# The start of a two-layer network: bias rows straight from the input, their loads on SyncE, flips first, values behind scores

## The chip, the cores and the metric

The kernel runs on one core of a Trainium2 chip. The metric is device time in microseconds (us); lower is better. In the engine names of the profile PE is TensorE, DVE is VectorE, ACT is ScalarE, POOL is GpSimd and SP is SyncE, which computes nothing and issues most of the DMAs.

## The reference

The input is an image batch `x` of shape (2, 128, 64, 64): two images, 128 channels, 64 x 64 pixels, float32. It goes through two layers.

```python
# layer 0: group norm, then a block with 7x7 neighbourhood attention
x = x + _L0_conv_ref(_gn(x), ...)
# layer 1: full attention over the 4096 tokens, then spectral convolutions
t = _to_tokens(x)
t = t + _L1_attn_ref(_ln_t(t))
t = t + _L1_ffn_ref(_ln_t(t), ...)
x = _from_tokens(t, x)
```

The change concerns the start of layer 0. Inside it:

```python
y = _ln(x, g1, be1)
qkv = (y @ qkv_w.T + qkv_b)...          # 4 heads of 32
attn = einsum('bnhwd,bnhwijd->bnhwij', q, Kw)   # 49 neighbours of each pixel
attn = attn + rpb[:, bih, biw]          # learned bias by relative position, one table a head
attn = softmax(attn)
out = einsum('bnhwij,bnhwijd->bnhwd', attn, Vw) @ proj_w.T + proj_b
y = _ln(out, g2, be2) @ w1.T + bl1;  x = y + r
y = relu(_ln(x, g3, be3) @ w2.T + bl2);  y = _ln(y, g4, be4) @ w3.T + bl3;  x = y + r
```

`rpb` is a table of 13 x 13 biases for each of the four heads; a pixel at the border has its neighbourhood shifted inside the image, so that the same table is read at other offsets there.

## The kernel before

**Bands.** Layer 0 works on 16 bands, eight per image; a band is 8 rows of 64 pixels, that is 512 tokens. In a band the 64 pixels of an 8 x 8 tile attend to a window of 14 x 14 pixels (196 keys) around it, with a mask for the pairs that are no neighbours. Two tiles make a unit, and a band has four units u0 to u3.

**Pieces.** The work of a band is cut into named pieces. The preparation pieces begin with `p.`: `xg` applies the group norm (L453), `tok` transposes to tokens on PE (L344), `bn`, `pw`, `nb`, `zd`, `za` make the layer norm, `tr` (L202) and `zT` (L445) turn the normed tokens back, `q` and `k` are linears on PE (L349) with their copies `qT` (ACT, L468) and `kT` (DVE, L477), and `v` (PE, L483) with its copy `vc` (ACT, L491) makes the values. A unit's pieces are `S`, the scores on PE (L523); `t0` to `t3`, per head the addition of the bias table together with a minimum on DVE (L536); `e0` to `e3`, the exponentials on ACT (L546); `T` and `c`, transposes of the probabilities (PE L559) and their copies (L566); and `V`, the product with the windows of the values (PE L581).

**Values through DRAM.** A window of 14 x 14 pixels reaches into neighbouring bands, so the values go through a DRAM buffer `vd`. The piece `vc` writes the band's eight tiles there (L493, eight DMAs of 32 KB), and `windows` reads, for every unit, four pieces of 98 pixels into a tile `vw` (L510, 49 KB each, six tiles in rotation). The windows of a band can be completed only when the next band's values are stored. All of these DMAs are issued by SP.

**Order.** The pieces have due times: a dictionary `PLAN` gives one to each piece name, and band k adds k * `PERIOD` (2300). The pieces are emitted in the order of due time. For the start there is a list `FIRST`: what stands in it gets its position minus 1000 as due time, so all of it comes ahead of u0.S of the first band (due at 0). Everything that PE, DVE, ACT and POOL do is then executed in the written order, each engine for itself; SP's DMAs are ordered by a scheduler, by when they can go. A ring of five PSUM banks serves linears, flips, values, scores and transposes in written order.

**The bias table.** The table comes in padded, as `rpb_pad`, with 22 rows of 70 numbers for each head. The kernel copies it to a DRAM scratch `rpb` that has six more rows ahead (two DMAs on ACT's queue, L306 and L307). It then loads, for each head, 64 partitions that start at consecutive offsets, 1350 numbers each, 337.5 KB in all (L310, `rev[h]`; four DMAs on ACT's queue; heads 0 and 3 lie in the space named `tt`, heads 1 and 2 in `cm`). `flipped(h)`, listed as f0 to f3, multiplies with a reversed identity to turn the order of partitions (PE L269, two products of 400 columns) and copies the result to `base` (ACT L273). `table` subtracts it from the mask: 196 keys per row, for six cases of border by four heads. The first case is done on DVE (tab0 to tab3, L278), the others on POOL (`tab`).

**The first loads.** SP loads image 0 in four parts (`xa`, L136), the weights (L284 to L286) and the mask (L301, 588 KB).

Layer 1 follows: attention from about 340 us to 1000 us, the convolutions from there to the end.

Of the kernel before, what the change touches and what calls it, by code (L numbers as in the profile page):

```python
# [8 lines left out]
F32 = mybir.dt.float32  # L9
AF = mybir.ActivationFunctionType  # L10
ALU = mybir.AluOpType
# [9 lines left out]
HEADS, DH, KW = 4, 32, 7  # L21
# [5 lines left out]
DIAG = -1.0e6  # L27
# [8 lines left out]
RPW = 70  # L36


QT, WN, NTAB = 8, 14, 20
# [5 lines left out]
RPR = NTAB + 2  # L45
RLEN = (NTAB - 1) * RPW + NTAB
# [25 lines left out]
PERIOD = 2300  # L72


FIRST = (
    "gn p.xg0 p.xg1 p.tok0 p.tok1 w f0 f1 p.bn0 p.bn1 p.pw0 p.pw1 x1 p.zd0 p.nb0 p.za0 p.tr0 p.zd1 p.nb1 p.za1 wd p.xg2"
    " p.zT0 f2 p.tr1 f3 tab p.zT1 p.v0 p.q0 p.k0 p.vc0 p.qT0 tab0 tab1 tab2 p.kT0 tab3 p.v1 p.k1 p.q1 p.vc1 p.kT1 p.qT1"
).split()
PHW = P + TH


# [21 lines left out]
def kernel(  # L103
# [16 lines left out]
    nc = tc.nc  # L120
# [4 lines left out]
    first_ = ExitStack()  # L125
# [9 lines left out]
    for c in range(4):  # L135
# [10 lines left out]
    space = tok[0].rearrange("p n c -> p (n c)")  # L146
# [3 lines left out]
    rev = [place[:, 0 : NTAB * RPW], *(cm[0][0 : QT * QT, h * RLEN : h * RLEN + NTAB * RPW] for h in range(2))]  # L150
    rev.append(place[:, NTAB * RPW : 2 * NTAB * RPW])

    ident = const.tile([P, P], F32, name="ident")
    make_identity(nc, ident)

# [3 lines left out]
        out=flip, in_=flip, compare_op=ALU.not_equal, fill=1.0, base=1 - QT * QT, pattern=[[0, 2], [1, QT * QT]],  # L159
        channel_multiplier=1,  # L160
    )
    ndiag = const.tile([P, P], F32, name="ndiag")
    nc.vector.tensor_scalar(ndiag, ident, DIAG, None, ALU.mult)
    ones = const.tile([1, P], F32, name="ones")
    nc.vector.memset(ones, 1.0)
    mhalf = const.tile([P, KF], F32, name="mhalf")
# [73 lines left out]
    with l0a:  # L240
# [10 lines left out]
        vdram = l0a.enter_context(tc.tile_pool(name="l0_dram", bufs=1, space=bass.MemoryType.DRAM))  # L251
# [3 lines left out]
        w_sb = wp.tile([P, 896], F32, name="w_sb")  # L255
        v_sb = wp.tile([P, 11], F32, name="v_sb")
        r_sb = wp.tile([1, 4, P], F32, name="r_sb")
# [4 lines left out]
        tab = big.tile([P, 6, HEADS, KEYS], F32, name="tab")  # L262
# [12 lines left out]
        def table(ci, h, eng):  # L275
# [5 lines left out]
                    base[hp, h, n0 : n0 + WN, m0 : m0 + WN], ALU.subtract,  # L281
                )

        nc.sync.dma_start(out=w_sb, in_=wT)  # L284
        nc.sync.dma_start(out=v_sb, in_=vecs)
        nc.sync.dma_start(out=r_sb, in_=rows.unsqueeze(0))  # L286


        gavg = wp.tile([P, 32, 4], F32, name="gavg")
        nc.gpsimd.memset(gavg, 0.25)  # L290
        nc.gpsimd.affine_select(
            out=gavg, in_=gavg, compare_op=ALU.is_ge, fill=0.0, base=0,
# [3 lines left out]
            out=gavg, in_=gavg, compare_op=ALU.is_ge, fill=0.0, base=3,  # L296
            pattern=[[4, 32], [0, 4]], channel_multiplier=-1,
        )
        gavg = gavg.rearrange("p g r -> p (g r)")

        nc.sync.dma_start(out=mask, in_=nc.inline_tensor(_window_masks(), "window_masks").ap())  # L301


        rpb = vdram.tile([(6 + HEADS * RPR) * RPW], F32, name="rpb")
        flat = rpb_pad.rearrange("h r w -> (h r w)")
        nc.scalar.dma_start(out=rpb[0 : 6 * RPW], in_=flat[0 : 6 * RPW])  # L306
        nc.scalar.dma_start(out=rpb[6 * RPW :], in_=flat)  # L307
        for h in range(HEADS):
            src = bass.AP(rpb.tensor, rpb.offset + h * RPR * RPW + 50, [[RPW, QT], [1, QT], [1, RLEN]])
            nc.scalar.dma_start(out=rev[h][:, 0:RLEN], in_=src)  # L310
        wg = w_sb
        cb = wp.tile([P, 5], F32, name="cb")
        C_Q, C_K, C_V, C_1, C_3 = range(5)
# [478 lines left out]
        for k, (b, g) in enumerate(order):  # L792
            t = {}
            for name, at in PLAN.items():
                if name[0] == "k" and b == 0:
                    continue

                at = FIRST.index(f"{name}{k}") - 1000 if f"{name}{k}" in FIRST else at + k * PERIOD
                events.append((at, k, name, lambda f=pieces[name], t=t, b=b, g=g: f(t, b, g)))
        def second():  # L800
            for c in range(4):
# [75 lines left out]
    with ap_:  # L877
# [6 lines left out]
        def bank():  # L884
# [6 lines left out]
            out=tr.rearrange("p h e c -> p (h e) c"),  # L891
            in_=nc.inline_tensor(t_in, "t_in").ap().rearrange("(h p) c -> p h c", p=P),
# [565 lines left out]
        for hh in range(SG // 2):  # L1458
            for e in range(2):
                at = 1 + (2 * hh + e) * 2 * LG * KF  # L1460
                pns[hh, e] = zc[0][:, 0, at : at + 2 * LG * KF].rearrange("p (k l f) -> p k l f", k=KF, l=2)
                nc.sync.dma_start(
                    out=pns[hh, e].rearrange("p k l f -> p (k l) f"),
                    in_=bass.AP(
                        phi_pad.tensor, P - FB + (2 * P * hh + e) * FB, [[2 * FB, P], [PHW, 2 * KF], [1, LG]]
                    ),
# [338 lines left out]
def _window_masks():  # L1805

    import numpy as np

    def seen(offset):

        q, k = np.arange(QT)[:, None], np.arange(WN)[None, :]
        lo = np.clip(offset + q - 3, 0, WN - KW)
        return (k >= lo) & (k < lo + KW)

    m = np.zeros((2, QT, QT, 6, WN, WN), np.float32)
    for ci in range(6):
        rows_ = seen((0, 6, 3)[ci // 2])
        for ab in range(2):
            cols = seen(((0, 6), (3, 3))[ci % 2][ab])
            m[ab, :, :, ci] = np.where(rows_[:, None, :, None] & cols[None, :, None, :], 0.0, -MASKED)  # L1820
    return m.reshape(P, 6, KEYS)
# [76 lines left out]
```

## Time and profile before

| what | value |
|---|---|
| median of the three runs shown | 1955.65 us (1949.8, 1955.65, 1957.53) |
| the profiled execution: its own time | 1954.66 us |
| the profiled execution: span | 1952.8 us |
| PE busy | 1891.0 us |
| layer 0, 0 to 340 us | PE busy 15.93 of the first 31 us, 146.91 of the 156 to 187, 147.11 of the 153 to 340 |
| attention, 340 to 1000 us | PE busy 651.86 of 660 us |
| convolutions, 1000 to 1952 us | PE busy 929.21 of 952 us |

The span is the time from the first to the last instruction that the profiler saw; the run's own time holds 1.9 us around it. A row of a timeline has the start in us, the duration, the engine, the line of the kernel, the operation, output<-input, sizes, and how many instructions were put together (x8); square brackets give the idle time just before and what ended it. "SPq" and "ACTq" are the issuing of DMAs by SP and ACT; a row there lasts as long as the issuing does, not as long as the transfer. "PEld" is the loading of weights into PE.

### The profile page before, as it was taken

The page shows a single profiled execution, that of the slowest core. Times are in us where ns is not written, and L with a number is a line of the kernel's source. Part 1 is how long each engine was busy: PE and PEld are TensorE (multiplying, and loading weights), DVE is VectorE, ACT ScalarE, POOL GpSimd, SP SyncE. Part 2 cuts the span into 40 slices and gives each one's busy share as a digit, 9 for nine tenths or more (in the row PEclk, how much of TensorE's full clock was granted, in tenths as well). Part 3 has the DMA queues.
Part 4 walks back from the last instruction along what each step waited for, and adds up shares of the span by engine and source line. Part 5 has one row for each costly group of instructions (what it writes and reads, how often), then busy time and mean ns, then how long its engine had stood idle before and what let it go on. Part 6 is the DMA issues. An engine that isn't in the chain of part 4 may idle for free.

```text
span 1952.8 us, 50772 instructions
## 1 busy us (share of the span) xinstructions
PE 1891.0 (97%) x20440; PEld 1347.5 (69%) x20440; DVE 956.0 (49%) x3026; ACT 731.3 (37%) x1718; POOL 737.7 (38%) x1209
## 2 busy tenths in 40 slices
PE   6899998999999999999999998999999999999997
PEld 3677776444444444444444456999999999999996
DVE  5799997454554534353454373333333333333332
ACT  2789887322233333232333222222222222222221
POOL 4366886424643335532425431122221121222211
PEclk9999999999999999999999999999999999999999
DMA  5222221667776544988867413222222223222211
GB/s 155 63 61 59 62 62 39 153 184 211 228 203 188 156 123 125 261 206 228 247 196 197 127 53 83 67 65 69 66 67 54 59 72 90 66 68 67 67 40 44
DMA packets 249769, 226.14 MB, mean 116 GB/s; under 512 B 126815, under 2 KB 204655, under 8 KB 242112
## 3 DMA queue, kind: packets, MB, share of 16 engines
q1 hardware_dynamic: 222786, 129.15, 27.5%
q10 hardware_dynamic: 8126, 58.04, 7.6%
q0 software_dynamic: 18624, 35.72, 6.3%
q8 instruction: 162, 2.65, 0.6%
q14 instruction: 71, 0.58, 0.1%
HBM read 131.40 MB, written 91.25 MB: 114 GB/s over the span
## 4 chain that ended last, share of the span: by engine, by line
PE 84%; DVE 5%; POOL 4%; DMA 2%; issue 1%; ACT 1%; SPq 0%; ACTq 0%; DVEq 0%; POOLq 0%
PE acc L1620 29%; PE own L984 12%; PE other L1057 9%; PE bank L926 9%; PE pc L1601 7%; PE bank L349 2%; PE bank L935 2%; PE bank L559 2%; PE bank L202 2%; PE bank L1177 1%; PE bank L1221 1%; PE bank L523 1%; ACT p L546 1%; PE po L581 1%; PE pc L1658 1%
## 5 line engine op out<-in xcount | busy, mean ns | idle before, releaser
L1606 DVE COPY y<-pc 128x512 f32<-128x512 f32 x320 | 206.2, 686 | 348.6 <-PE pc L1601 348.3
L1606 ACT COPY y<-pc 128x512 f32<-128x512 f32 x320 | 171.8, 589 | 402.5 <-PE pc L1601 396.9
L1620 PE MATMUL acc<-y,mpl 32*128 32x256 f32 x5120 | 321.6, 379 | 0.8 <-DVE af L1630 0.8
L1620 PE MATMUL acc<-y,mmi 32*128 32x256 f32 x5120 | 313.1, 375 | 0.0
L1620 PEld LDWEIGHTS acc<-y,mpl 32*128 32x128 f32 x5120 | 289.4, 186 | 7.3 <-DVE af L1630 1.7
L1620 PEld LDWEIGHTS acc<-y,mmi 32*128 32x128 f32 x5120 | 290.4, 185 | 2.6
L1631 POOL TENSOR_TENSOR af<-af 128x512 f32<-128x512 f32 x39 | 49.7, 1274 | 573.3 <-DVE af L1630 535.9
L1057 PE MATMUL other<-e,tok 128*128 128x512 f32 x448 | 227.5, 594 | 0.2
L931 ACT ACTIVATE e<-bank 128x512 f32<-128x512 f32 x216 | 129.1, 598 | 252.5 <-PE bank L926 241.8
L926 PE MATMUL bank<-cm 128*128 128x512 f32 x432 | 222.5, 601 | 0.0
L984 PE MATMUL own<-et,tok 128*128 128x512 f32 x448 | 212.1, 598 | 3.3 <-DVE et L974 3.2
L1601 PE MATMUL pc<-ct,ut 32*128 32x256 f32 x2560 | 208.3, 376 | 2.0 <-DVE y L1606 2.0
L1162 POOL TENSOR_TENSOR ub<-uo 128x256 f32<-128x256 f32 (+1 forms) x176 | 111.0, 666 | 176.4 <-ACT uo L1158 148.2
L1601 PEld LDWEIGHTS pc<-ct,ut 32*128 32x128 f32 x2560 | 170.1, 185 | 7.6 <-DVE y L1606 4.1
L974 DVE STREAM_TRANSPOSE et<-et 128x512 f32<-128x512 f32 x216 | 134.2, 678 | 70.9 <-DMA et<-eb 70.8
L984 PEld LDWEIGHTS own<-et,tok 128*128 128x128 f32 x448 | 85.7, 192 | 111.2 <-issue 96.1
L1057 PEld LDWEIGHTS other<-e,tok 128*128 128x128 f32 x448 | 81.5, 191 | 89.6 <-issue 82.1
L926 PEld LDWEIGHTS bank<-cm 128*128 128x128 f32 x432 | 76.3, 191 | 73.9 <-issue 67.7
L546 ACT ACTIVATE p<-p,mn 128x196 f32<-128x196 f32 x256 | 114.3, 449 | 14.4 <-DVE mn L536 13.9
L1093 POOL DMA_DIRECT2D us<-ub x158 | 108.0, 725 | 12.5 <-DMA us<-ub 10.1
L1158 ACT COPY uo<-bank 128x512 f32<-128x512 f32 (+1 forms) x96 | 45.4, 517 | 96.9 <-PE bank L1177 55.2
L1630 DVE COPY af<-acc 128x256 f32<-128x256 f32 x80 | 30.3, 420 | 104.6 <-PE acc L1620 104.6
(269 smaller groups left out, 2625.3 us busy)
## 6 DMA issues: line engine op xcount, KB each, us to landing
eb<-e ACTq DMA_DIRECT2D x54, 1024.0 KB
et<-eb SPq DMA_DIRECT2D x216, 256.0 KB
ut<-us SPq DMA_DIRECT2D x156, 128.0 KB
us<-ub POOLq DMA_DIRECT2D x54, 256.0 KB, 5.2
vw<-vd SPq DMA_DIRECT2D x256, 49.0 KB
ct<-gs SPq DMA_DIRECT2D x312, 40.0 KB
ct<-gs SPq DMA_DIRECT2D x312, 32.0 KB
vd<-v SPq DMA_DIRECT2D x128, 32.0 KB
```

The source lines that it names most:

```text
L546: nc.scalar.activation(p, p, AF.Exp, bias=t[name + "mn"][:, h : h + 1], scale=-1.0, accum_out=t["den"][:, u, h : h + 1],)
L926: nc.tensor.matmul(ps.rearrange("p (q t j) -> p q t j", q=4, t=4), lhsT=cm[b][:, n * P : (n + 1) * P], rhs=keys.rearrange("p (t q j) -> p ...
L931: nc.scalar.activation(e, ps.rearrange("p (q t j) -> p q t j", q=4, t=4), AF.Exp, bias=0.0, scale=ASCALE)
L974: in_place(nc.vector.transpose(part, part))
L984: nc.tensor.matmul(out_, lhsT=tok[b][:, n, :], rhs=e, start=first, stop=last, skip_group_check=True)
L1057: nc.tensor.matmul(turn(other, "p (q t j) -> p q t j"), lhsT=tok[b][:, n, :], rhs=es[j], start=(j == 0), stop=(j == 3),)
L1093: by.dma_start(out=to, in_=part)
L1162: adder[sgn].tensor_tensor(ub[:, sgn, 0:n], both[:, 0:n], both[:, n : 2 * n], op)
L1601: nc.tensor.matmul(pcs[j].rearrange("p (g o c) -> p o g c", g=4, o=2)[:, :, at], lhsT=ut[rows_, par, :], rhs=cv_[rows_], start=True, stop= ...
L1606: (nc.scalar.copy if j % 2 else nc.vector.tensor_copy)(y[:, :, :, 4 * kl + j, :], pcs[j].rearrange("p (g x k) -> p k g x", g=4, k=KF))
L1620: nc.tensor.matmul(acc[j][:, 0:256], lhsT=(mmi if l else mpl)[rows_, k, :], rhs=y[rows_, k, 2 * l : 2 * l + 2].rearrange("p s n x -> p (s ...
L1631: eng.tensor_tensor(af[:, 0:2], af[:, 0:2], af[:, 2:4], ALU.add)
```

## The change

The list `FIRST` is written anew. Flip 1 comes ahead of the weight products, flips 0 and 3 behind them, flip 2 behind the first transposes; k comes before q in band 0; the normed second band stands a little later. The values of the first two bands leave the list and get due times of their own (`BEHIND`), just behind the scores u0.S of band 0.

The scratch `rpb` now holds only what head 0 needs, in a DRAM pool of its own that is opened earlier, so its two writes on ACT's queue are smaller. The rows of heads 1 to 3 are read from `rpb_pad` itself, where the rows ahead belong to the head before. All four loads of rows are issued by SP, among its other first loads: head 1, the weights, heads 0, 3 and 2, and the mask last. A constant `ndiag` is made by ACT instead of DVE.

```diff
 FIRST = (
-    "gn p.xg0 p.xg1 p.tok0 p.tok1 w f0 f1 p.bn0 p.bn1 p.pw0 p.pw1 x1 p.zd0 p.nb0 p.za0 p.tr0 p.zd1 p.nb1 p.za1 wd p.xg2"
-    " p.zT0 f2 p.tr1 f3 tab p.zT1 p.v0 p.q0 p.k0 p.vc0 p.qT0 tab0 tab1 tab2 p.kT0 tab3 p.v1 p.k1 p.q1 p.vc1 p.kT1 p.qT1"
+    "gn p.xg0 p.tok0 p.xg1 p.tok1 f1 w p.bn0 p.pw0 p.bn1 f0 p.pw1 p.zd0 p.nb0 p.za0 f3 p.zd1 p.nb1 p.tr0 p.za1 wd f2"
+    " p.zT0 p.tr1 x1 p.k0 p.zT1 p.q0 tab0 p.kT0 p.qT0 p.k1 p.q1 p.xg2 tab p.kT1 p.qT1 tab1 tab3 tab2"
 ).split()
+BEHIND = {"p.v0": 1, "p.v1": 2, "p.vc0": 3, "p.vc1": 4}
...
+    rpb = rdram.tile([(6 + RPR) * RPW], F32, name="rpb")
+    flat_ = rpb_pad.rearrange("h r w -> (h r w)")
+    nc.scalar.dma_start(out=rpb[0 : 6 * RPW], in_=flat_[0 : 6 * RPW])
+    nc.scalar.dma_start(out=rpb[6 * RPW :], in_=flat_[0 : RPR * RPW])
...
-    nc.vector.tensor_scalar(ndiag, ident, DIAG, None, ALU.mult)
+    nc.scalar.activation(ndiag, ident, AF.Identity, bias=0.0, scale=DIAG)
...
-        nc.sync.dma_start(out=w_sb, in_=wT)
-        nc.sync.dma_start(out=v_sb, in_=vecs)
-        nc.sync.dma_start(out=r_sb, in_=rows.unsqueeze(0))
...
+        def rows_of_head(h):
+            if h:
+                tensor, at = rpb_pad.tensor, rpb_pad.offset + (h * RPR - 6) * RPW
+            else:
+                tensor, at = rpb.tensor, rpb.offset
+            nc.sync.dma_start(
+                out=rev[h][:, 0:RLEN], in_=bass.AP(tensor, at + 50, [[RPW, QT], [1, QT], [1, RLEN]])
+            )
+
+        rows_of_head(1)
+        nc.sync.dma_start(out=w_sb, in_=wT)
+        nc.sync.dma_start(out=v_sb, in_=vecs)
+        nc.sync.dma_start(out=r_sb, in_=rows.unsqueeze(0))
+        for h in (0, 3, 2):
+            rows_of_head(h)
         nc.sync.dma_start(out=mask, in_=nc.inline_tensor(_window_masks(), "window_masks").ap())
...
-        rpb = vdram.tile([(6 + HEADS * RPR) * RPW], F32, name="rpb")
-        flat = rpb_pad.rearrange("h r w -> (h r w)")
-        nc.scalar.dma_start(out=rpb[0 : 6 * RPW], in_=flat[0 : 6 * RPW])
-        nc.scalar.dma_start(out=rpb[6 * RPW :], in_=flat)
-        for h in range(HEADS):
-            src = bass.AP(rpb.tensor, rpb.offset + h * RPR * RPW + 50, [[RPW, QT], [1, QT], [1, RLEN]])
-            nc.scalar.dma_start(out=rev[h][:, 0:RLEN], in_=src)
...
-                at = FIRST.index(f"{name}{k}") - 1000 if f"{name}{k}" in FIRST else at + k * PERIOD
+                at = FIRST.index(f"{name}{k}") - 1000 if f"{name}{k}" in FIRST else BEHIND.get(f"{name}{k}", at + k * PERIOD)
```

More of the change, by code (lines that the diff above doesn't have):

```diff
@@ L151 @@
     rev.append(place[:, NTAB * RPW : 2 * NTAB * RPW])
+    rdram = first_.enter_context(tc.tile_pool(name="rpb", bufs=1, space=bass.MemoryType.DRAM))
+    rpb = rdram.tile([(6 + RPR) * RPW], F32, name="rpb")
+    flat_ = rpb_pad.rearrange("h r w -> (h r w)")
+    nc.scalar.dma_start(out=rpb[0 : 6 * RPW], in_=flat_[0 : 6 * RPW])
+    nc.scalar.dma_start(out=rpb[6 * RPW :], in_=flat_[0 : RPR * RPW])
     ident = const.tile([P, P], F32, name="ident")
```

## The prediction, made before the changed kernel was run

> **What bounds the kernel now.** I read the busy shares first, then the chain that ended last.
>
> ```profile
> PE 1891.0 (97%) x20440; PEld 1347.5 (69%) x20440; DVE 956.0 (49%) x3026; ACT 731.3 (37%) x1718; POOL 737.7 (38%) x1209
> ...
> PE 84%; DVE 5%; POOL 4%; DMA 2%; issue 1%; ACT 1%; SPq 0%; ACTq 0%; DVEq 0%; POOLq 0%
> ```
>
> PE is the bound on average. The change touches only the first 60 us, so what counts is whether a shift there reaches the end of layer 0 (about 340 us); layer 1 then follows on a PE that is never free. The page counts no DMA-issuing time, so I read the timeline of SP's own queue (start, duration, line, count):
>
> ```profile
> 8.64 0.35 SPq L301 DMA_DIRECT2D tok<-window_masks  x1
> 31.47 9.98 SPq L493 DMA_DIRECT2D vd<-v  x16
> 41.50 17.21 SPq L510 DMA_DIRECT2D vw<-vd  x22
> 58.80 4.96 SPq L493 DMA_DIRECT2D vd<-v  x8
> 63.86 13.11 SPq L510 DMA_DIRECT2D vw<-vd  x16
> 77.06 4.96 SPq L493 DMA_DIRECT2D vd<-v  x8
> ...
> 118.17 12.64 SPq L510 DMA_DIRECT2D vw<-vd  x16
> ```
>
> Idle before, from 31.47 on SP starts each row where the last one ends. SP stores a band's values to DRAM (8 issues, 4.96 us, 0.62 each) and loads its windows (16 issues, 12.64 us, 0.79 each): 17.6 us of issuing per band, and a band comes every 17.8 to 19 us (77.06 to 58.80 is 18.26). So SP is as full as PE. SP really waits only where a row is longer than its usual time: 13.11 against 12.64 is 0.47, and two more such places before 187 (13.09 at 99.92, 5.28 at 148.72) make 1.2 us in all.
>
> Does PE wait for SP? The chain between 176 and 215 us says so at the first band of the second image:
>
> ```profile
> 191.64 0.79 SPq L510
> ...
> 194.13 0.73 SPq L510
> 194.91 2.55 DMA vw<-vd
> 197.50 0.32 PE po L581 x8
> ```
>
> The product with the values (L581) begins when the window of the fifth issue has landed, 2.55 us after that issue began (194.91). Elsewhere the margin is small: the windows of a band's first unit are completed by the fifth issue behind its row of stores. Behind 113.11 that issue starts near 121.4 (118.17 + 4 x 0.79), lands near 124.0, and PE's row of that product starts at 124.36: 0.4 us to spare. Bands 1 to 6, read likewise, have 0.4 to 1.3 us. Hence a later start of SP reaches PE nearly in full.
>
> **What sets SP's start.** It is the copy of the first band's values (ACT L491). The rows that lead to it:
>
> ```profile
> 14.12 2.14 PE L344 MATMUL bank<-ident,xg 128*128 128x128 f32 x8 [1.28 <-DVE xg L453]
> ...
> 17.77 1.70 PE L269 MATMUL bank<-tt,flip 64*128 64x400 f32 x2
> 20.63 1.70 PE L269 MATMUL bank<-cm,flip 64*128 64x400 f32 x2 [1.16 <-DMA cm<-rpb]
> ...
> 28.75 2.07 PE L483 MATMUL bank<-w_sb,zT 128*128 128x128 f32 x8
> 30.62 3.20 PE L349 MATMUL bank<-zT,w_sb 128*128 128x512 f32 x4
> 33.66 1.05 PE L483 MATMUL bank<-w_sb,zT 128*128 128x128 f32 x8
> 34.55 1.88 PE L349 MATMUL bank<-zT,w_sb 128*128 128x512 f32 x4
> ```
>
> The seven rows are tokens, flip 0, flip 1, v0, q0+k0, v1, k1+q1. The same linear costs 1.6 us in the first pair and 0.94 in the second: PE's clock changes near 33.3. Then:
>
> ```profile
> 30.86 0.58 ACT L491 COPY v<-bank 128x512 f32<-128x512 f32 x1 [1.02 <-PE bank L483]
> ...
> 35.78 0.88 DVE L477 TENSOR_SCALAR kT<-bank,cb 128x128 f32<-128x128 f32 x2
> ...
> 37.99 0.33 DVE L536 CUSTOM_DVE_ANT_0 p<-bank,tab 128x196 f32<-128x196 f32 x1
> ...
> 38.36 0.46 ACT L546 ACTIVATE p<-p,mn 128x196 f32<-128x196 f32 x1 [1.21 <-DVE mn L536]
> ```
>
> **The change, part by part.**
>
> *The loads.* The four row loads leave ACT's queue and are issued by SP as head 1, weights, 0, 3, 2, mask; only head 0 still goes through scratch. Moved issues: four at about 0.4 to 0.7 us, in a time when SP has nothing else, while ACT's table load moves ahead of them. A head lands in about 2.8 us: 337.5 KB, of which the DMA view of 15 to 18 us shows 0.37 MB moved per 3 us on half of the engines. Queued from 8.8 on I estimate head 1 at 11.6, weights 12.8, head 0 at 15.6, head 3 at 18.4, head 2 at 21 to 24, mask 23.6 to 26.5. Before, PE waited 1.16 for a row load at 20.63; that goes. Next late would be head 2 (flip 2 in PE's order at 24.2) and the mask (first table at 28.6); neither is. The moved constant (one DVE operation to ACT) and the smaller scratch store cost nothing: both lie before the group norm's tokens at 14. POOL's order is unchanged; its tables need all four flips, copied by 26.4 instead of 29.4.
>
> *The order on PE.* Tokens end at 16.15. From the rows: flip 1 to 17.85, weight products (1.9) 19.75, flip 0 21.4, flip 3 23.05, transposes of band 0 (1.1) 24.15, flip 2 25.8, transposes of band 1 26.9. Flips run one behind another without the 1.16 wait and without the pauses ahead of each transpose. Then k0 28.6, q0 30.2 (1.6 cold), k1 31.35, q1 32.3 (the clock goes full on the way; I take 30.7), tokens 2 at 32.9. First scores L523 at 32.9 instead of 36.80: 3.9 earlier.
>
> *Scores' consumers.* kT1 (DVE) is done at 32.3, but now three table pairs (3 x 1.07) and the statistics of band 2 (1.1) stand behind it and ahead of the first addition L536: 32.3 + 3.2 + 1.1 = 36.6, against 37.99. The values of band 1 take the bank of the first scores, freed by that addition, so their copy ends near 38.6, and it stands ahead of the first exponential on ACT: 38.6 against 38.36. PE's own chain through the exponentials is thus +0.25, its 3.9 us spent.
>
> *Values behind scores.* Scores end at 33.5, v0's products (1.05) at 34.55, the copy (0.58) at 35.15. Before it ended at 31.44. So SP starts 3.7 us later. In the built order 17 windows instead of 22 precede the third band's stores, so these start near 58.5 as before (35.2 + 10.0 + 13.3) and band 1 isn't late; but the five windows left follow behind them, and from the fourth band's stores on SP is the whole 3.7 late. Bounds: a clock full from 27 on gives +2.1; cold products throughout (q0, k1, q1 at 1.6, scores 0.95, v0 2.07) give +6.6.
>
> *What arrives at the end.* SP's three waits (1.2 us) can absorb part of the delay, since SP was ahead of its data there; between 0 and 1.2 I take 0.7, about half, because PE shifts along from band 2 on and so keeps part of them. At 187 the band is already late for SP, and behind it PE is busy 89.32 of 90 us (187 to 277), so nothing is won back. Sum: 1954.66 (the profiled run's own time, span 1952.8) + 3.7 - 0.7 = 1957.7. The median of the runs, 1955.65, lies 1.0 above the profiled run.
>
> [...] The rows above show SP's issues back to back. [...] Here an issue of 0.79 us stands against 2.55 us to landing, but landings overlap and issues don't; I go by the rows.
>
> **Rivals.**
>
> A. *The end follows PE, not SP.* For it: the margins of 0.4 to 1.3 us could widen, as PE's half clock (granted 0.50 to 0.51 from 40 to 52 us) hides SP in the first band. Against: 194.91. Between the exponentials' +0.25 and the first scores' -3.9 it gives 1951 to 1955.
>
> B. *Slower by over 0.5%.* The row loads now share one queue with the mask, behind the input. If each packet took the 0.56 us that the first ones took near 9.5 us, not the 0.33 of the later ones, a head would need 4.8 us (2.8 x 0.56 / 0.33): head 1 at 13.6, weights 15, head 0 at 19.8, head 3 at 24.6, head 2 at 29.4, mask at 33 or later. The first table, with kT0, the tokens of band 2 and kT1 behind it on DVE (1.1 + 0.9 + 0.7 + 0.9), would hold the scores until 36.6 and v0's copy until 38.8; each further 1 us of the mask adds 1 us. A copy at 40 to 44 gives 1962 to 1966.5, and it passes 0.5% from a copy at 42.9 on (11.5 late, less 0.7). Against: near 9.5 all engines were still busy with the input, by 15 half of them were free.
>
> C. *Nothing moves* (the reorder cancels: SP +3.7 less its waits 1.2, less up to 2 us of a first band that ends sooner as the half-clock stretch begins earlier): 1954.5 to 1956.
>
> **How the numbers follow.** Main 0.55, A 0.25, B 0.10, C 0.10. The main case's bounds, +2.1 - 1.2 and +6.6, give 1955.5 to 1961.3; runs shown lie within 4 us of the median on both sides; A reaches down to 1951, B to 1967. The range leaves out the last of each: 1951 to 1965. A change of 0.5% (9.8 us) is about what a measurement of this kernel can tell from none. Faster than 1945.9 needs A and more: 0.04. Slower than 1965.4 is B's upper part (0.06) and a main case with the spread of the runs on top (0.04): 0.10. Same: 0.86.
>
> **What would show it.** Right: SP's first store near 35.1, then no gap until 277; scores near 33 and the first L536 near 36.6; first exponential 38.4; the first L581 of the second image still ended by a window, near 200. Wrong: gaps in SP's queue while PE's products start before 197.5 (A); the flip of head 2 or the first table waiting for DMA (B); v0's copy before 33.6 (clock sooner full).

## The result and the profile after

The changed kernel takes 1957.79 us (median of 21 runs, 1952.27 to 1964.94), the kernel before 1952.21 us over as many runs: a ratio of 1.0026, 95% interval 1.0018 to 1.0034, so some 5 us more, and within the half per cent that the forecast called no change. The predicted time was 1957.7. The profiled execution of the changed kernel has a span of 1956.2 us, against 1952.8 before.

The queue of SP, from the timeline of the changed kernel (start, duration, engine, line; L501 are the stores of the values, L518 the windows):

```profile
9.92 0.45 SPq L318 DMA_DIRECT2D tok<-window_masks  x1
34.68 10.15 SPq L501 DMA_DIRECT2D vd<-v  x16
44.88 13.31 SPq L518 DMA_DIRECT2D vw<-vd  x17
58.55 4.97 SPq L501 DMA_DIRECT2D vd<-v  x8
63.63 17.00 SPq L518 DMA_DIRECT2D vw<-vd  x21
80.73 4.97 SPq L501 DMA_DIRECT2D vd<-v  x8
85.81 12.64 SPq L518 DMA_DIRECT2D vw<-vd  x16
98.55 6.16 SPq L501 DMA_DIRECT2D vd<-v  x8
```

The first store comes at 34.68 instead of 31.47 (3.2 late), the third band's at 58.55 (before 58.80), the fourth band's at 80.73 instead of 77.06: 3.7 late, as the order of the queue had it. The row at 98.55 is 1.2 us longer than its like; one single store in it took 1.77 us.

The rows of PE and ACT behind it:

```profile
14.81 2.15 PE L352 MATMUL bank<-ident,xg 128*128 128x128 f32 x8 [1.28 <-DVE xg L461]
16.88 1.70 PE L276 MATMUL bank<-cm,flip 64*128 64x400 f32 x2
...
20.39 3.03 PE L276 MATMUL bank<-tt,flip 64*128 64x400 f32 x4
...
27.17 4.82 PE L357 MATMUL bank<-zT,w_sb 128*128 128x512 f32 x8
...
32.36 0.59 PE L531 MATMUL bank<-kT,qT 32*64 32x196 f32 x16
32.87 1.16 PE L491 MATMUL bank<-w_sb,zT 128*128 128x128 f32 x8
37.27 2.08 PE L491 MATMUL bank<-w_sb,zT 128*128 128x128 f32 x8 [3.24 <-DVE mn L544]
```

```profile
34.07 0.58 ACT L499 COPY v<-bank 128x512 f32<-128x512 f32 x1 [1.35 <-PE bank L491]
39.38 0.58 ACT L499 COPY v<-bank 128x512 f32<-128x512 f32 x1 [4.73 <-PE bank L491]
39.87 0.46 ACT L554 ACTIVATE p<-p,mn 128x196 f32<-128x196 f32 x1
```

The flips run without the wait of 1.16, the first scores begin at 32.36 (before 36.80), and nothing comes of it: the values of band 1 wait 3.24 us on PE for their bank, then run at a granted clock of 0.54 (36 to 40 us; 2.08 us instead of 1.05), and the first exponential starts at 39.87, 1.5 later than before. The values of band 1 matter to SP as well: their copy ends at 39.96, and the last eight of the sixteen first stores (4.96 us of issuing) cannot be issued ahead of it. So the first windows, at 44.88, start when this second copy lets them.

The first unit of image 1 (L589 is the product with the values), from PE's timeline of the changed kernel, and from that of the kernel before:

```profile
200.56 0.54 PE L589 MATMUL po<-pT,vw 98*32 98x64 f32 x24
202.26 0.32 PE L589 MATMUL po<-pT,vw 98*32 98x64 f32 x8 [1.16 <-DMA vw<-vd]
```

```profile
196.51 0.54 PE L581 MATMUL po<-pT,vw 98*32 98x64 f32 x24
197.50 0.32 PE L581 MATMUL po<-pT,vw 98*32 98x64 f32 x8 [0.44 <-DMA vw<-vd]
```

The last eight matmuls wait for the window, 4.8 us later than before. The windows of this band begin at 196.44 on SP, where they began at 191.64 before: SP is 4.8 us late there, and so is PE. PE's waits between 60 and 340 us show less of it, 2.1 us for windows where it was 0.4 in the kernel before, because PE came to this window late by itself: 0.6 us at band 1, and 1.2 and 1.3 in two stretches of slow clock near 81 and 101 (granted 0.50 from 82 to 84 and from 102 to 104). The landing of the window at 202.2 is SP's work; an earlier PE would have waited longer for it.

```profile
PE po L589 <- DMA vw<-vd: 2.1, 3, 1.2
```

```profile
PE po L581 <- DMA vw<-vd: 0.4, 1, 0.4
```

### The profile page after: what moved, and what is told of

Its sections match the earlier page's. It is cut to its first block, busy times and chain, and to the rows that moved or that the text cites. A ratio compares the mean times of both kernels' runs of the same rounds, so it can differ in the third digit from the quotient of the medians.

```text
span 1956.2 us, 50771 instructions
## 1 busy us (share of the span) xinstructions
PE 1892.4 (97%) x20440; PEld 1350.1 (69%) x20440; DVE 956.0 (49%) x3025; ACT 731.7 (37%) x1719; POOL 738.3 (38%) x1209
## 4 chain that ended last, share of the span: by engine, by line
PE 83%; DVE 6%; POOL 4%; DMA 2%; ACT 2%; SPq 2%; issue 1%; DVEq 0%; POOLq 0%; ACTq 0%
PE acc L1628 29%; PE own L992 12%; PE other L1065 9%; PE bank L934 9%; PE pc L1609 7%; PE bank L357 2%; PE bank L943 2%; PE bank L1185 1%; PE bank L209 1%; PE bank L567 1%; PE bank L1229 1%; ACT p L554 1%; SPq L501 1%; SPq L518 1%; PE pc L1666 1%
## 5 line engine op out<-in xcount | busy, mean ns | idle before, releaser
L934 PE MATMUL bank<-cm 128*128 128x512 f32 x432 | 222.5, 601 | 0.0
L934 PEld LDWEIGHTS bank<-cm 128*128 128x128 f32 x432 | 76.2, 191 | 74.0 <-issue 68.4
L554 ACT ACTIVATE p<-p,mn 128x196 f32<-128x196 f32 x256 | 114.4, 449 | 12.9 <-DVE mn L544 12.5
```

The source lines that it names most:

```text
L554: nc.scalar.activation(p, p, AF.Exp, bias=t[name + "mn"][:, h : h + 1], scale=-1.0, accum_out=t["den"][:, u, h : h + 1],)
L934: nc.tensor.matmul(ps.rearrange("p (q t j) -> p q t j", q=4, t=4), lhsT=cm[b][:, n * P : (n + 1) * P], rhs=keys.rearrange("p (t q j) -> p ...
```

## The experiments

Theory S says that SP's queue is full from the first store on, so that the late copy of the first values reaches the end. Rival P says that the end follows PE's first 60 us, rival L that the first loads count. Ratios are to the kernel before, with 95% intervals; 0.1% are 2 us.

**SP late, nothing else.** The kernel before with five more stores ahead of the first ones:

```diff
             nc.scalar.copy(v.rearrange("p j c -> p (j c)"), t["pv"])
+            for i in range(5 if (b, g) == (0, 0) else 0):
+                nc.sync.dma_start(out=more[i], in_=v[(i % 2) * 64 : (i % 2 + 1) * 64, i // 2, :])
             for i, c in enumerate(TILES):
```

> Kernel before with five more stores of the first band's values (to a spare place that nobody reads) issued by SP ahead of the real ones; nothing else moves. They delay SP's real stores by 5 x 0.62 = 3.1 us. Theory S (SP's queue carries its delay to the end): +2.5 to +5 us over before, the V of the first unit of image 1 (197.5 in before) at 200 to 202.5. Rival P (the end follows PE's first scores and exponentials): no change, within 1 us. Rival L (the changed first loads): no change.

Ratio 1.0026 (1.0012 to 1.0039), 5 us, the same as the whole change. The rows of SP in it:

```profile
30.30 3.10 SPq L494 DMA_DIRECT2D more<-v  x5
33.45 9.94 SPq L496 DMA_DIRECT2D vd<-v  x16
```

In this execution the copy itself was 1.2 us sooner than in the profile before, so the first unit of image 1 had its windows at 199.6, 2.2 later than before, just short of the 200 expected. PE's and ACT's orders are untouched: SP's lateness alone costs what the change costs. P and L fall as the whole cause. The 5 us stand on the medians (1958.17 of 12 runs against 1953.7 of 35); the profiled execution is one of the fastest (1954.53) and shows 2.2 of them up to image 1, so where the rest is lost is not shown.

**Values in front.** The changed kernel with the values of both bands back in the list:

```diff
-    " p.zT0 p.tr1 x1 p.k0 p.zT1 p.q0 tab0 p.kT0 p.qT0 p.k1 p.q1 p.xg2 tab p.kT1 p.qT1 tab1 tab3 tab2"
+    " p.zT0 p.tr1 x1 p.v0 p.k0 p.zT1 p.vc0 p.q0 tab0 p.kT0 p.qT0 p.v1 p.k1 p.vc1 p.q1 p.xg2 tab p.kT1 p.qT1 tab1 tab3 tab2"
...
-BEHIND = {"p.v0": 1, "p.v1": 2, "p.vc0": 3, "p.vc1": 4}
+BEHIND = {}
```

> Changed kernel with the values of the first two bands put back ahead of k and q in the list; the new loads and the flips' order stay. v0's copy should end near 29.8 (tr1 26.9 + cold products 2.07 + copy 0.58 + 0.3) instead of 34.65: SP starts 4.9 us sooner than in the changed kernel, 1.6 sooner than before. Theory S: 3.5 to 6 us less than the changed kernel, that is 0 to 2 us under before. Rival L: stays 3 to 5 us over before. Rival P: first scores come some 3 us later than in the changed kernel, so the time is not under the changed kernel's.

The ratio is 0.9994 (0.9979 to 1.0009), the median 1952.35. SP's first store stands at 29.23 (5.5 sooner than in the changed kernel), and the first unit of image 1 has its windows at 196.05, 0.3 ahead of PE. The loss is gone while the loads and the flips' order stay: L falls. SP is 2.2 ahead of before here, of which no gain is measurable.

**Values behind, nothing else.** The kernel before with only the two entries moved:

```diff
-    " p.zT0 f2 p.tr1 f3 tab p.zT1 p.v0 p.q0 p.k0 p.vc0 p.qT0 tab0 tab1 tab2 p.kT0 tab3 p.v1 p.k1 p.q1 p.vc1 p.kT1 p.qT1"
+    " p.zT0 f2 p.tr1 f3 tab p.zT1 p.q0 p.k0 p.qT0 tab0 tab1 tab2 p.kT0 tab3 p.k1 p.q1 p.kT1 p.qT1"
 ).split()
+BEHIND = {"p.v0": 1, "p.v1": 2, "p.vc0": 3, "p.vc1": 4}
```

> Kernel before with only the values of the first two bands moved behind the first scores; loads and flips as before. PE is free of 3.1 us of value products ahead of the scores, so these come near 34, v0's copy near 35.7 instead of 31.44: SP 4.2 late. Theory S: +3.5 to +6 us over before, as much as the whole change or a little more. Rival L: 0. Rival P: scores sooner by 2 to 3 us, so 0 to 3 us under before.

The ratio is 1.0040 (1.0027 to 1.0053), 7.8 us, above the 6 expected and more than the delay of SP (first store at 36.30, 4.8 late). The chain of this kernel and its windows show where the rest comes from:

```profile
91.84 2.56 DMA vw<-vd
94.44 0.44 PE po L582 x8
94.89 2.01 PE bank L350 x2
96.89 1.71 PE bank L560 x8
98.60 1.43 PE bank L484 x8
```

```profile
88.00:92.00 4.00, 2.18 (x32) 1.04 (x29) 2.26 (x5) 2.60 (x9) 2.43 (x2) 1.00 0.19 52
92.00:96.00 4.00, 1.55 (x10) 0.87 (x11) 0.00 (x0) 0.00 (x0) 0.00 (x1) 0.60 0.22 61
96.00:100.00 4.00, 4.00 (x25) 3.20 (x23) 1.75 (x9) 1.27 (x2) 0.29 (x2) 0.55 0.25 74
```

PE waits up to 94.44 for the windows of band 2 (busy 1.55 of 4 us, third entry of the second row), and the granted clock, the third number from the end, goes to 0.60 and 0.55 in that stretch. Two linears then take 2.01 instead of 1.06. Behind PE's two waits for these windows (1.37 and 2.90 us) the last three rows of the chain take some 2.3 us more than their like at full clock (2.01 + 1.71 + 1.43 against 1.06 + 0.87 + 0.89). So the moved values alone cost at least what the whole change costs. That they cost more, and that the new loads and order give some of it back, fits the copy of the first values (it ends 1.6 us sooner in the changed kernel, 34.65 against 36.27), but the two intervals overlap.

**Five first stores on ACT.**

```diff
-                nc.sync.dma_start(
+                (nc.scalar if (b, g) == (0, 0) and i > 2 else nc.sync).dma_start(
```

> Changed kernel in which five of the first band's eight stores are issued by ACT, which idles 4.7 us there, the other three by SP. SP's queue is 5 x 0.62 = 3.1 us shorter; PE's order and everything else stay. Theory S: 2.5 to 4.5 us less than the changed kernel, within 2 us of before. Rivals P and L: no change against the changed kernel (within 1 us).

The ratio is 1.0029 (1.0016 to 1.0043): nothing is gained, and what theory S expected did not come. SP's rows say why:

```profile
33.66 10.43 SPq L501 DMA_DIRECT2D vd<-v  x11
44.13 14.85 SPq L518 DMA_DIRECT2D vw<-vd  x19
```

Eleven stores took as long as sixteen (10.43 us against 10.15): the eight of band 1 wait for their own copy, which ends at 39.2, so the windows begin at 44.13 as they would have anyway (44.88 in the changed kernel, where that copy ends at 39.96). The change has two late copies; taking one out of the queue does not help. The run tells nothing against S, but my working had left the second copy out.

**Three stores of a band on POOL.** This was done on the changed kernel, on the kernel before, on the one with values in front, and on that one with PE kept busy. The edit is the same, from the third band on (14 bands, so 42 stores, not the 36 that the first expectation counts):

```diff
-                nc.sync.dma_start(
+                (nc.gpsimd if i > 4 and (b or g > 1) else nc.sync).dma_start(
```

> Changed kernel in which, from the third band on, three of a band's eight stores are issued by POOL instead of SP. The start is that of the changed kernel: v0's copy near 34.7, the first window load near 44.9. SP then has 1.9 us less to issue per band (of 17.6), so it makes up its 3.4 us within two or three bands. Theory S: PE's waits for windows end after band 3, and the time is 3 to 6 us under the changed kernel, from 2 under to 2 over before. Rival P (PE's first 60 us carry the loss): it stays 4 to 6 us over before. A cost of its own: POOL issues 36 stores, some 0.7 us each by its other DMA rows, and its tables and statistics wait for the copies; if that decides, the time is over that of the changed kernel.

> Kernel before with the same three stores per band on POOL from the third band on. Theory S: SP is no longer the last at the first band of image 1 (it was by 0.9 us), and not near it elsewhere: 1 to 3 us under before. Rival P: no change, or slower by what POOL's issuing costs.

> New loads and flips, values of the first two bands in front (as in the second experiment), and three stores per band on POOL from the third band on. Theory S: SP starts 2 us sooner than in before and has room afterwards; what is left is PE: 2 to 5 us under before, and no wait of PE for a window in image 1. Rival: the second experiment was already bound by PE, so the same as that one.

The fourth has the following behind the first scores as well:

```diff
+                if (b, g, u) == (0, 0, 0):
+                    idle = ps_o.tile([P, 4, P], F32, tag="po", name="po")
+                    for _ in range(4):
+                        nc.tensor.matmul(
+                            idle.rearrange("p j c -> p (j c)"), lhsT=wg[:, W_QKV : W_QKV + P], rhs=t["p.zT"],
+                            start=True, stop=True,
+                        )
```

> The kernel of the seventh experiment with four linears of 512 columns (0.94 us each at full clock) more behind the first scores, whose results nobody reads; they fill the 3.75 us in which PE idled there and after which its clock was granted at one half from 37 to 53 us. If the idle time causes the half clock, the clock is 0.9 or more from 34 to 42, and the first V (52.9 in the second experiment) comes 2 to 6 us sooner. Theory S: the first windows are then the limit (they land at 45 to 55), and of the gain 1 to 3 us arrive at the end. Rival P: all of it arrives, 3 to 6 us.

All four take 2027 to 2029 us: 1.0398 (1.0382 to 1.0414), 1.0388 (1.0368 to 1.0408), 1.0387 (1.0372 to 1.0403) and 1.0384 (1.0363 to 1.0405). PE's waits in the first of them, between 60 and 420 us, and POOL's timeline:

```profile
PE bank L352 <- POOL xg L461: 52.7, 26, 2.9
```

```profile
80.20 1.79 POOL L501 DMA_DIRECT2D vd<-v  x3 [12.50 <-ACT v L499]
82.03 2.43 POOL L461 TENSOR_SCALAR xg<-xa,gm,grs 128x128 f32<-128x128 f32 x2
```

POOL's stores wait for the copy of the values (12.5 us idle ahead of them), and the group norm of the next band stands behind them in POOL's order; PE needs that one. The cost that the first of these expectations had named as possible decided. In the first of them a band's first window lands 9.6 to 12.4 us ahead of PE in bands 2 to 6 and in the first six bands of image 1, so SP is out of the way, and the start that differs between these kernels makes no difference (2028.73 and 2028.0 for values behind and in front). With POOL as the limit this says little about S.

**Stores on ACT and on POOL at a better place.** Two per band on ACT, on the changed kernel:

```diff
-                nc.sync.dma_start(
+                (nc.scalar if i > 5 and (b or g > 1) else nc.sync).dma_start(
```

> Changed kernel in which, from the third band on, the last two of a band's eight stores are issued by ACT right behind its own copy of the values (no wait of another engine is added). SP has 1.2 us less per band, so the 3.4 us of its late start are made up by the fifth band. Theory S: PE's waits for windows in image 1 end and the time is 2.5 to 5.5 us under the changed kernel. The cost is at most 1.2 us of ACT per band ahead of eight exponentials; if PE waits for these (rival E), the time is up to 15 us over before.

Three per band on POOL, but in a piece of its own behind `xg`, on the changed kernel and on the one with values in front:

```diff
+    "p.vs": -2380,
...
+        @piece("p.vs")
+        def _(t, b, g):
+            if pooled(b, g):
+                stores(b, g, t["v"], nc.gpsimd, range(8 - pooled(b, g), 8))
+                wanted(b, g)
```

> Changed kernel with three of a band's stores on POOL from the third band on, as in the fifth experiment, but written behind POOL's group norm xg of the next band instead of ahead of it. If the 75 us came from xg waiting behind stores that wait for the copy, they go: PE's wait for xg is under 3 us in layer 0 (it was 52.7). Theory S then: 2 to 6 us under the changed kernel. If POOL's stores themselves are slow to land, the windows wait for them and the time is over the changed kernel's.

> The same stores on POOL behind xg, with the values of the first two bands in front (as in the second experiment) and the new loads and flips. Theory S: SP starts 2 us sooner than in before and has 1.9 us of room per band: 1 to 5 us under before. If PE alone is the bound there, as in the second experiment: 0 to 2 under before.

They take 1.0064 (1.0050 to 1.0079), 1.0068 (1.0049 to 1.0087) and 1.0057 (1.0041 to 1.0073), medians 1965.51, 1964.85 and 1964.92: all slower than the changed kernel, the predicted gains missed. PE's waits between 60 and 340 us in the ACT kernel, then in the second and third alike:

```profile
PE bank L357 <- ACT zT L453: 11.3, 11, 1.5
PE bank L567 <- ACT p L554: 4.4, 5, 1.0
```

```profile
PE bank L352 <- POOL rb L624: 12.8, 9, 2.4
```

No row for windows is left; in all three a band's first window lands about 3 us or more ahead of PE from band 3 on. The waits for `xg` are gone as expected; `rb`, the next one in POOL's order, takes their place (12.8 us, 3.3 in the changed kernel), and on ACT it is `zT` and the exponentials (rival E). Two or three stores cost each engine more than SP's lateness had cost. And the two POOL kernels, which differ by the values behind or in front of the scores, differ by 0.1 us in their medians, where the changed kernel and the one with values in front differ by 5.4 (0.32% by their ratios). With room in SP's queue the place of the first values does not show, as far as these intervals (0.2%) can tell. That agrees with S but does not prove it, since the waits for `rb` could hide a difference too.

**PE kept busy, values in front.** The four linears from above, all stores on SP:

> The second experiment's kernel (new loads and flips, values in front, all stores on SP) with the four unread linears behind the first scores, which in the eighth experiment kept PE's clock full until 44 us. PE reaches the first product with the values some 3 us sooner than the 52.9 of the second experiment. Theory S: SP's queue is unchanged and its windows had 1 to 2 us to spare at bands 1 to 6 and 0.3 at the first band of image 1, so PE runs into the windows and at most 1 us arrives at the end: within 2 us of the second experiment. Rival P: 3 us or more under it.

The ratio is 0.9996 (0.9981 to 1.0011), the median 1951.81 us against 1952.35 without them. The windows of this kernel, with the granted clock third from the end:

```profile
34.00:38.00 4.00, 4.00 (x28) 1.95 (x27) 3.87 (x17) 0.69 (x1) 0.55 (x2) 1.00 0.25 57
38.00:42.00 4.00, 3.31 (x25) 2.11 (x31) 2.58 (x15) 2.46 (x9) 3.70 (x4) 1.00 0.19 48
```

and of the one without them:

```profile
34.00:38.00 4.00, 0.63 (x18) 0.23 (x16) 3.88 (x18) 0.63 (x2) 0.79 (x3) 0.85 0.22 51
38.00:42.00 4.00, 3.19 (x13) 2.55 (x13) 2.34 (x12) 2.40 (x10) 3.35 (x3) 0.50 0.22 55
```

The clock stays full at least until 42, and the first product with the values begins at 50.88 instead of 52.88. Then PE runs into SP:

```profile
PE po L596 <- DMA vw<-vd: 2.5, 2, 2.2
```

What is left there of the 2 us won in the first band, 1.2 us, is waited away at the first band of image 1, whose window lands at 197.9. In this execution that one transfer took 3.72 us from its issue at 194.16 instead of 2.5, so more was lost than had been won; at 2.5 it would have landed at 196.7, when the same eight matmuls began without the linears (196.7). A gain on PE's side of the start does not arrive, as S says; rival P wanted 3 us.

No version tried is clearly faster than the kernel before; two are level with it.

## Why the prediction was right

*What bounds.* This was right: a full queue of SP, margins near 1 us at each band, and a late start that reaches PE. The added stores (+5), the values in front (-5.4 against the changed kernel) and the filled idle time (no gain) show it from three sides.

*The loads.* It was right that they hide: neither the flip of head 2 (24.40) nor the first table waits for DMA, so rival B's slow queue did not come. What the prediction did not see is that the first tokens come at 14.81 instead of 14.12. The executions with the new loads differ there: in six of ten, the changed kernel's among them, the first tokens start at 14.39 to 14.81, in the other four at 13.96 to 14.15, and with the old loads all four start at 14.04 to 14.12. So the new loads seem to cost up to 0.7 us in some executions, which the prediction put at nothing; what of it reaches SP is not shown (the first store stands at 34.69 in an execution with tokens at 13.96). With the values in front the new loads cost nothing that could be measured.

*The order on PE.* Scores were said for 32.9 and came at 32.36, v0's copy was said for 35.15 and ended at 34.65; SP was 3.2 late instead of 3.7, since the matmuls got short a little sooner: the four linears ahead of the scores took 4.82 us, where the working has 5.4. The working calls that PE's clock, which is read off times alone: the granted clock reads 1.00 ahead of it too (20 to 34 us in both profiles), but a 128x128 transpose takes 421 ns at 23 to 27 us of the kernel before, as at 49 where 0.50 is granted, and 273 at 67 to 87 where 1.00 is. The sum's largest term holds, though the copy of band 1, which it left out, sets the first windows as much as the one of band 0 does.

*Scores' consumers.* The mechanism was right, but its size was off: the first addition was said for 36.6 and came at 36.88, but the values of band 1 cost 2.08 instead of 1.05: behind the 3.24 us that PE waited for their bank the granted clock was 0.54 (36 to 40 us; with the linears of the last experiment in such a wait it was 1.00 up to 42). The first exponential was 1.5 late instead of 0.25. It did not reach the end: the windows of band 0 land 3.8 to 5.6 us ahead of PE, the stores of the third band are on time, and the first unit of band 1 was 0.6 later than before (70.80 against 70.17).

*What arrives at the end.* This step failed in its parts and came out near by chance. I took 0.7 off for three places where SP waits. Two of them are waits, of 0.44 us (ahead of the issue at 74.59) and 0.35 us (150.97), and they are in the changed kernel as well, 0.52 us (75.89) and 0.42 us (153.81): SP lost there what it had lost before, and nothing was won back. The third, the row at 99.92, is no wait; two single issues in it last 0.94 and 1.02 us. Such issues of 0.9 to 1.8 us stand in both profiles near 100, 170 and 235 to 245 us. In place of a gain there was a loss: one of them took 1.2 us more at 102, and the first unit of image 1 was 4.8 later than before, not 3.0.

Behind image 1's start the slow clock moved the difference to and fro. Some 1.4 us came back behind band 14, where the profile of before has a clock of 0.57 (316 to 320 us) and that of the changed kernel a full one (1.00). As much was lost again at the end of layer 0 (0.51 from 340 to 345 us in the changed kernel, 0.95 before): the first products of attention (L926 before, L934 after) begin at 351.4 and 356.3 us. Some 1.7 came back near the end of attention (0.72 from 908 to 920 us before, 0.87 after), whose last products begin at 1091.6 and 1094.8. So the spans differ by 3.4. The medians differ by 5.6, since the profiled execution of before lies 2.4 above its median (1954.66 against 1952.21). The forecast of 1957.7 started from that execution and added 3.0; against the median the addition should have been some 5. The three runs that were known did not tell: their median, 1955.65, lies 3.4 above that of the 21 runs, and they lie within 5.9 us of it, not the 4 of the working.

*The slow clock.* The sum held no term for it after the start. In the third experiment it added 2.3 us behind PE's waits for windows (granted 0.60 and 0.55). In the changed kernel PE's clock fell near 81 and near 101, behind a wait of 1.18 us for `rb` that the kernel before has too, there without a fall (1.00 from 74 to 102 us):

```profile
78.00:82.00 4.00, 2.12 (x12) 1.85 (x13) 3.02 (x14) 3.32 (x12) 2.82 (x5) 0.83 0.22 64
82.00:86.00 4.00, 3.73 (x61) 2.71 (x60) 3.56 (x9) 2.29 (x6) 1.94 (x4) 0.74 0.27 63
```

Stretches of 2 us place the falls: 0.67, 0.50 and 0.98 from 80 to 86 us, and 0.79, 0.50 and 0.86 from 100 to 106. With 0.50 in a fall and 1.00 around it, each lasted some 3.4 us and began at 80.7 and at 101.1. In as long a stretch ahead of them PE was busy for 1.36 and 1.80 us. The busy time alone does not decide it: in the kernel before, 1.78 us in the 3.4 from 77.64 on brought no fall (1.00 from 80 to 86). What decides it is not shown here. Whether later stalls make such falls likelier on average or only shift them stays open; one execution of each can't tell. It would fit the excess of the medians over SP's 3.2.

*Issuing beside landing.* For one DMA the issuing is short (0.79 us against 2.55 us to landing in the kernel before), but a band has 24 of them, 17.6 us of issuing. Five issues of 0.62 us more, and nothing else, cost 5 us.

## What to carry to other kernels

The engine that issues DMAs can be full without showing as busy (here 17.6 us of issuing in a band of 17.8 to 19): add up its issues per stage and compare them with the stage's length. Where it is full, the moment of its first issue can count for more than that of the first scores (here the one came 3.2 us later, the other 4.4 sooner, and the time rose by 5), so what feeds it goes first and everything else behind it. Before issues are given to another engine, look at what that engine would hold back while it waits for the data: two or three stores a band made the kernel some 12 us slower than the one before, and 75 where a piece that PE needs stood behind them.

## What the runs showed that was not expected

POOL and ACT, busy 38% of the time on average, had no room for two or three stores per band in their written order: PE waited 13 to 16 us for their pieces, where the kernel before has 1.2 us for `zT` and 3.3 for `rb`. Stretches with PE busy for about half of 4 us were followed by either clock: 2.12 of 4 us busy (0.83), then 0.74 (changed kernel at 82 to 86); 1.97 of 4 us busy (kernel before, 76 to 80), then 1.00. With four unread linears (3.7 us of PE) in idle time the clock read 1.00 from 34 to 42 us, 0.90 and 0.50 in the next two stretches of 4 us (without them 0.85, then 0.50 from 38 to 50), and they cost nothing that could be measured (0.9996 with them, 0.9994 without). Single DMA issues of SP take up to 1.8 us (1.77 in the changed kernel, 1.71 in the kernel before) instead of 0.6 to 0.8 now and then; what causes this was not tried.
